# Cross attention on one core: scores by Strassen's seven products, sums of probabilities on GpSimd, and a new order of the step

## The chip, the core and the metric

The kernel runs on one core of a Trainium2 chip. The core has TensorE (PE) for matrix products, VectorE (DVE), ScalarE (ACT) and GpSimd (POOL) for elementwise work, and SyncE (SP), whose queue issues most DMAs. Each engine takes its instructions in order from a queue of its own and waits on semaphores that other engines raise. PE's results go to PSUM, which this program divides into eight banks of 128 x 512 f32; DVE and ACT read them there, and POOL works on SBUF alone. The metric is the device time of one execution in microseconds (us), smaller is better.

## The reference

The reference is one layer of a perceiver: cross attention from 8 x 64 queries to 8 x 1601 context rows, then self attention, then a feed-forward layer with weights quantised to three levels. The change lies in the cross attention, and the rest is untouched.

```python
def xattn(hidden, context, Wq, Wk, Wv, Wo, gq, gk):      # hidden 8x64x512, context 8x1601x256
    q = rmsnorm((hidden @ Wq).reshape(B, Sq, 16, 128), gq)
    k = rmsnorm((context @ Wk).reshape(B, Skv, 16, 128), gk)
    v = (context @ Wv).reshape(B, Skv, 16, 128)
    scores = einsum("bqhd,bkhd->bhqk", q, k) / sqrt(128)
    out = einsum("bhqk,bkhd->bqhd", softmax(scores), v)
    return out.reshape(B, Sq, 2048) @ Wo

x = x + xattn(layernorm(x), ctx, ...)
x = x + self_attention(layernorm(x), ...)                 # 16 heads of 32, causal
x = x + ffn(layernorm(x), ...)                            # ternary weights, 2048 hidden
```

## The kernel before

**What is computed in place of the keys.** The keys are never kept. For each head the weights of the keys are multiplied into the queries beforehand, so that a head's scores are the context (256 wide) times a matrix `a_sb` (256 x 64 for one batch and head), divided by the root of the mean square of each key. That root is the only thing for which the keys themselves are computed. Their product, context times Wk, is made by Strassen's algorithm in Winograd's form: the 256 context rows of a step and the 256 columns of the context are cut in halves, as are the 1024 columns of Wk that belong to eight heads, and seven products of 128 x 128 by 128 x 512 take the place of eight. The products need sums of the blocks of the context (`cxS`, s1 to s4, made on POOL at L204 to L207) and of the weights (`wkS`, t1, t2, t3 and n4, made once on POOL).

**Units and steps.** A unit `u` is one batch and one group of eight heads: 16 units. A unit has six steps `q` of 256 context rows each, and a tail of 65 rows that belongs to step 5. `step(u, q)` does, for its 256 rows, the seven products of the keys (`product`, L509), the squares and their sums on ACT (`squares`, L513, sixteen of 128 columns), and the scores of both tiles of 128 rows (`scores`, L478: two matmuls of 512 columns for each tile; rows on the partitions, 8 heads x 64 queries on the free axis). A step's scores are scaled by the roots at the start of the next step (`scale_pair`, put by in `later`): DVE multiplies PSUM into a tile `s` (L490) and keeps a running maximum `mx` (L499).

**The softmax lags one unit behind.** In step 0 of unit u the maxima of unit u-1 are reduced over the partitions (`find_max`: transposes L562, reduce L564) and spread to all of them by a matmul with ones (`spread_diag`, `spread_max`, L110, L556). In steps 1 to 4 (`PROBS`) each of its 13 tiles has the maximum taken off on DVE (`less_max`, L570), is exponentiated on ACT (`exponentials`, L575) and added to `den` on DVE (`add_to_sums`, L584). In step 5 the sums are spread (`find_sum`, `spread_sum`, L613) and inverted (`invert_sums`, L617). PE multiplies the tiles by the context rows into two banks `y0` and `y1` (`weigh`, `weigh_context`, L596: two matmuls of 512 columns for each tile), a few tiles later; `finish` (L623) scales the result into `a_sb`, over the queries that are no longer needed.

**What sets the order.** Inside the steps the order of PE, DVE and ACT is the order in which `step` calls, because they stand in a manual schedule. POOL and SP are ordered by the framework's scheduler. Waits follow from tiles: a writer of a buffer waits for its last reader. PSUM has these tags: `k` (two banks, p_u and p_5), `m` (two, p_2 and what is transposed or spread), `s` (two, scores), `y0` and `y1`.

The keys' products share banks. p_u is written by the first product, copied out on ACT as p1 (L718), added to by the third product and copied out as u2 (L746), added to again, read by DVE for c22 (L774), and added to a last time; p_5 is written, copied out as p5 (L743), added to and read by DVE for c12 (L803). Each of these readers has to end before PE adds to the bank again.

**Side work in the steps.** Every second step also quantises one tile of the feed-forward weights: a load `wf`, two passes on ACT (`magnitudes`, L426 and L428), five instructions on DVE at the end of the step (`quantise`, L434 to L445), three more one step later (`signed`, L451 to L453), then a DMA transpose and a store. `transpose_context` turns the context of a later step on DVE (L190) and makes its sums on POOL. `load_context` brings the rows for `weigh`, with six buffers (`CXN`). In unit 0, which has no softmax behind it, PE computes in place of `weigh` the keys' roots of the tail rows (`key_roots`: matmul L245, squares `ksq` on ACT, reduce on DVE L254).

**Before the steps** (`qphase`): the context tails are loaded in one DMA and transposed (L368), the tails' key roots of group 0 computed, x normalised and transposed, the queries computed head by head (L332) and `a_sb` formed (L358). Only PE is in a manual schedule there. **After the steps**: the last unit's softmax and `weigh`, values and projection, self attention and feed-forward.

Of the kernel before, what the change touches and what calls it, by code (L numbers as in the profile page):

```python
# [14 lines left out]
ALU = mybir.AluOpType  # L15
# [13 lines left out]
def perceiver_kernel(  # L29
# [123 lines left out]
    CXN = 6  # L153
# [14 lines left out]
    def load_blocks(b, q):  # L168

        t = ctxp.tile([P, NC, 8, 32], F32, tag="cxB", name="cxB", bufs=3)  # L170
        src = cx[b, 2 * q * P : 2 * (q + 1) * P, :].rearrange(
            "(ki kj) (c ci cj) -> ci kj c ki cj", kj=32, c=NC, cj=32
        )
        for i in range(4):
            nc.sync.dma_start(t[32 * i : 32 * i + 32], src[i])
        cxB[b, q] = t
# [7 lines left out]
    def transpose_context(b, q):  # L184
# [4 lines left out]
        t = ctxp.tile([P, NC, 2 * P], F32, tag="cxT", name="cxT", bufs=7)  # L189
# [8 lines left out]
        if (b, q) == (0, 0):  # L198
            sums = ctxp.tile([P, 4, P], F32, tag="cxB", name="cxS", bufs=3)
        else:  # L200
            sums = work.tile([P, 4, P], F32, tag="og", name="cxS", bufs=HG)
# [23 lines left out]


# [3 lines left out]
    def load_tails(qp):  # L230
        t = qp.tile([P, B, C], F32, tag="wq3", name="cxt")
        nc.sync.dma_start(
            t[:TAIL], cx[:, NJF * P :, :].rearrange("b k c -> k b c")
        )
        return t

    def key_roots(ct, g, kr, new_kp, new_ksq):
# [3 lines left out]
        ssq = small.tile([P, HG], F32, tag="ssq", name="ssq")  # L241
# [16 lines left out]
    def tail_roots(i, g, new_kp, new_ksq):  # L258
# [3 lines left out]
        kr = small.tile([P, HG], F32, tag="krt", name="krt")[: n1 - n0]  # L262
# [10 lines left out]
    with tc.tile_pool(name="qphase", bufs=1) as qp, tc.tile_pool(  # L273
# [36 lines left out]
        for q in range(2):  # L310
# [4 lines left out]
        nc.vector.scalar_tensor_tensor(  # L315
            gqk, gq_t, float(HD) ** -0.5, gk_t, ALU.mult, ALU.mult
        )
        wkT, qraw, qr = {}, {}, {}

        def transpose_wk(h):  # L320

            g, hg = divmod(h, HG)
            tp = ps.tile([P, NC, P], F32, tag="tp", name="tp_wk")
# [39 lines left out]
        with tc.manual_schedule(engines={mybir.EngineType.PE}):  # L363

            for b in range(B):
                tp = ps.tile([P, NC, P], F32, tag="tp", name="tp_cx")
                for c in range(NC):
                    nc.tensor.transpose(  # L368
                        tp[:, c, :TAIL], cxt[:TAIL, b, ts(c, P)], ident[:TAIL, :TAIL]
                    )  # L370
                (nc.scalar.copy if b % 2 else nc.vector.tensor_copy)(
                    cxP[:, :, b, :], tp[:, :, :TAIL]
                )
            load_wq(3)
            for i in range(n_tails):
                for _ in tail_roots(
# [4 lines left out]
                ):  # L381
                    pass
                if i > 0:
                    t = i - 1
                    xn = normalise(x_sb, t, qp)
                    tp = ps.tile([P, ND, P], F32, tag="tp", name="tp_ln")
                    for c in range(ND):
                        nc.tensor.transpose(tp[:, c, :], xn[:, ts(c, P)], ident)
                    nc.scalar.copy(xT[:, :, ts(t, P)], tp)
# [22 lines left out]
    def load_weights(u):  # L412
# [7 lines left out]
        wf = fq.tile([P, 512], F32, tag="wf", name="wf", bufs=2)  # L420
# [43 lines left out]
    s_sb, mx, mB, den, rB, yps = {}, {}, {}, {}, {}, {}  # L464
# [4 lines left out]
    def scores(u, j):  # L469
        b, g = divmod(u, G)  # L470
        r = rows(j)
        sp = ps.tile([P, HG, S], F32, tag="s", name="sp")
        for c in range(NC):
            if j < NJF:
                ct = cxT[b, j // 2][:, c, ts(j % 2, P)]
            else:
                ct = cxP[:, c, b, :]
            nc.tensor.matmul(  # L478
                sp[:r],
                ct,  # L480
# [4 lines left out]
        return sp  # L485

    def scale_scores(u, j, sp, kr):
        r = rows(j)
        s = work.tile([P, HG, S], F32, tag="s", name="s", bufs=16)
        nc.vector.tensor_tensor(  # L490
            s[:r], sp[:r], kr[:r].unsqueeze(2).to_broadcast([r, HG, S]), ALU.mult
        )
        s_sb[u, j] = s

# [6 lines left out]
    def bank(tag, name):  # L501
        return ps.tile([P, 4 * HD], F32, tag=tag, name=name)
# [44 lines left out]
    def spread(parts):  # L547

        bp = ps.tile([P, W], F32, tag="m", name="bp")
# [8 lines left out]
    def find_max(u):  # L558
        tp = ps.tile([P, W // P, P], F32, tag="m", name="tp_mx")
# [7 lines left out]
    def less_max(u, j):  # L567
        r = rows(j)
        s = s_sb[u, j]
        nc.vector.tensor_tensor(s[:r], s[:r], mB[u][:r], ALU.subtract)  # L570

    def exponentials(u, j):
        r = rows(j)
        s = s_sb[u, j]
        nc.scalar.activation(s[:r], s[:r], AF.Exp, bias=zero_t[:r], scale=1.0)  # L575

    def add_to_sums(u, j):
        r = rows(j)
        s = s_sb[u, j]
        if j == 1:  # L580
            den[u] = work.tile([P, HG, S], F32, tag="t2", name="den", bufs=12)
            nc.vector.tensor_tensor(den[u], s_sb[u, 0], s, ALU.add)
        elif j > 1:
            nc.vector.tensor_tensor(den[u][:r], den[u][:r], s[:r], ALU.add)  # L584

    def weigh_context(u, j):
# [7 lines left out]
        s = s_sb.pop((u, j))  # L594
        for c in range(NC):
# [51 lines left out]

    def load_wo(h):
        wo_sb[h] = work.tile([P, D], F32, tag="s", name="wo", bufs=16)
# [32 lines left out]
    PROBS = {1: range(0, 3), 2: range(3, 6), 3: range(6, 10), 4: range(10, NJ)}  # L682
# [12 lines left out]
    def step(u, q):  # L695
# [6 lines left out]
        b11, b21, b22, t1, t2_, t3, n4 = wkS[g]  # L702
        ssq = small.tile([P, 2, HG], F32, tag="ssq2", name="ssq2")
        probs = PROBS.get(q, ()) if u > 0 else ()
        sp, fw_tile = [], None
# [4 lines left out]
        p_u = bank("k", "p_u")  # L710
        product(p_u, a11, b11, True)
        if q != 1:
            for j in probs:
                less_max(u - 1, j)
        if u > 0 and q == 5:
# [3 lines left out]
        while later:  # L719
            later.pop(0)()  # L720
        if q == 1:
            for j in probs:
                less_max(u - 1, j)
# [11 lines left out]
        early = q != 1  # L735
        for j in probs[:early]:
            exponentials(u - 1, j)


        p_5 = bank("k", "p_5")  # L740
# [6 lines left out]
        for j in probs[early:]:  # L747
            exponentials(u - 1, j)
        for _ in roots:
            pass  # L750
        if u > 0 and q != 1:
            weigh(1)
        if q == NQU - 1:
            tail = scores(u, NJF)
            if u > 0:
                spread_sum(u - 1)
            scale_scores(u, NJF, tail, krP[:, b, ts(g, HG)])
        if u > 0 and q == 0:
            find_max(u - 1)
        if q % 2 == 0 and n_q < NQ:  # L760
            fw_tile = magnitudes(wf)


        c11, c22 = kept("c11"), kept("c22")

        def product_2():
            p_2 = bank("m", "p_2")
            product(p_2, a12, b21, True)
            nc.vector.tensor_tensor(c11, p_2, p1, ALU.add)
            squares(ssq[:, 0], 0, c11)  # L770

        def product_7():
            product(p_u, s3, t3, False)
            nc.vector.tensor_tensor(c22, p_u, p5, ALU.add)  # L774
            squares(ssq[:, 1], 1, c22)

        if u > 0 and q == 1:
            product_2()
            sp.append(scores(u, 2 * q))
            product_7()  # L780
        else:
            product_7()
            product_2()
            sp.append(scores(u, 2 * q))
        for j in probs:
            add_to_sums(u - 1, j)
        if u > 0 and q == 1:
            weigh(1)
        if u > 0 and q == 0:
            mB[u - 1] = spread_diag(mB[u - 1])  # L790
# [3 lines left out]
        if n_tp < len(pairs) and turn_at[n_tp] == u * NQU + q:  # L794
            transpose_context(*pairs[n_tp])
            n_tp += 1


# [537 lines left out]
```

## Time and profile before

| | |
|---|---|
| Median of 3 runs | 1744.43 us (1741.65 to 1745.04) |
| The profiled execution | 1742.82 us, of it 1741.0 us from the first to the last instruction |
| Granted TensorE clock | 0.997 on the mean |
| PE busy | 1715.9 us, 99% |
| DVE busy | 1186.6 us, 68% |
| ACT busy | 1069.9 us, 61% |
| POOL busy | 133.6 us, 8% |
| First product of the first step | at 127.2 us |

A row of a group or a timeline names the line of the program, the engine and operation, the tile that is written and those that are read, the shape and the count. In a timeline the first column is the start and the second the length from the first instruction's start to the last one's end, in us, and what stands in brackets is the idle time of the engine before it and what ended it. DVE and ACT start the next instruction some 0.08 to 0.10 us before the last one's recorded end. A matmul's recorded length is longer than the distance to the next matmul's start, because matmuls are pipelined; distances between starts are what counts. In the view of windows the columns are the window, the busy time of each engine with its count of instructions, the granted TensorE clock, and the DMA's share and rate.

### The profile page before, as it was taken

To read this page: it belongs to the slowest core of one execution; us is meant where nothing else is said; L and a number is where in the kernel's file an instruction comes from. 1 tells how busy PE (TensorE), PEld (TensorE's weight loads), DVE (VectorE), ACT (ScalarE), POOL (GpSimd) and SP (SyncE) were. 2 spreads that over 40 slices of the span, in tenths; PEclk is the share of its full clock that TensorE was granted. 3 is DMA by queue.
4 is the path that set the end of the run, shared out by engine and by line. 5 is a ranking of instruction groups with operands and counts; after the bars stand their busy time and mean duration, and the time that the engine had idled before them with its cause. 6 is when DMAs were issued, how large, how long until landed. Compare 5 with 4: busy or idle time off the path is not lost.

```text
span 1741.0 us, 17756 instructions
## 1 busy us (share of the span) xinstructions
PE 1715.9 (99%) x4712; PEld 825.6 (47%) x4712; DVE 1186.6 (68%) x2007; ACT 1069.9 (61%) x4274; POOL 133.6 (8%) x234
## 2 busy tenths in 40 slices
PE   8999999999999999999999999999999999999898
PEld 3444344444444444444444444444444444466687
DVE  4446687878787878778787878787778776145431
ACT  4447676767676776767676768676777663023441
POOL 2001100000000000000000000000000000100031
PEclk9999999999999999999999999999999999999999
DMA  6102121212121122121212212121121226400330
GB/s 194 25 7 43 37 54 45 57 39 54 46 60 46 42 57 47 49 50 46 57 40 54 53 43 57 41 59 45 46 51 31 64 50 229 132 1 1 97 97 25
DMA packets 189222, 98.76 MB, mean 57 GB/s; under 512 B 135593, under 2 KB 167873, under 8 KB 189121
## 3 DMA queue, kind: packets, MB, share of 16 engines
q1 hardware_dynamic: 182593, 85.04, 19.0%
q0 software_dynamic: 6240, 12.58, 2.8%
q8 instruction: 38, 0.62, 0.2%
q14 instruction: 63, 0.52, 0.1%
q10 hardware_dynamic: 288, 0.00, 0.0%
HBM read 77.62 MB, written 7.34 MB: 49 GB/s over the span
## 4 chain that ended last, share of the span: by engine, by line
PE 96%; ACT 2%; DVE 1%; DMA 0%; issue 0%; SPq 0%; ACTq 0%; DVEq 0%
PE y L596 21%; PE sp L478 20%; PE p_u L509 19%; PE p L509 14%; PE gu L1205 3%; PE qps L332 3%; PE op L671 3%; PE kp L245 2%; PE fop L1273 2%; PE mm_qk L990 2%; PE vp L656 2%; PE aps L358 1%; PE bp L110 1%; PE mm_v L1008 1%; ACT e L1051 1%; PE mm_p L1097 1%
## 5 line engine op out<-in xcount | busy, mean ns | idle before, releaser
L513 ACT ACTIVATE c<-c 128x128 f32<-128x128 f32 x1152 | 339.7, 296 | 104.9 <-DVE c L774 78.5
L596 PE MATMUL y<-s,cxn 128*128 128x512 f32 (+1 forms) x832 | 389.1, 592 | 0.1
L478 PE MATMUL sp<-a,cxT 128*128 128x512 f32 x768 | 360.8, 592 | 0.0
L596 PEld LDWEIGHTS y<-s,cxn 128*128 128x128 f32 (+1 forms) x832 | 158.0, 190 | 199.1 <-issue 195.9
L478 PEld LDWEIGHTS sp<-a,cxT 128*128 128x128 f32 x768 | 145.8, 190 | 178.0 <-issue 172.6
L513 ACT ACTIVATION_READ_ACCUMULATOR c<-c 128x1 f32 x1152 | 215.3, 187 | 0.0
L490 DVE TENSOR_TENSOR s<-sp,ssq 128x512 f32<-128x512 f32 x192 | 130.0, 685 | 50.1 <-ACT ssq L105 49.2
L575 ACT ACTIVATE s<-s,zero_t 128x512 f32<-128x512 f32 (+1 forms) x208 | 140.0, 716 | 7.8 <-DVE s L570 6.5
L570 DVE TENSOR_TENSOR s<-s,mB 128x512 f32<-128x512 f32 (+1 forms) x208 | 134.7, 701 | 2.1 <-ACT mB L556 2.1
L584 DVE TENSOR_TENSOR den<-den,s 128x512 f32<-128x512 f32 (+1 forms) x176 | 121.2, 689 | 12.7 <-ACT s L575 0.2
L499 DVE TENSOR_TENSOR mx<-mx,s 128x512 f32<-128x512 f32 (+1 forms) x176 | 121.7, 692 | 6.1
L513 ACT ACTIVATE p_u<-p_u 128x128 f32<-128x128 f32 x384 | 100.5, 262 | 31.4 <-PE p_u L509 22.3
L743 ACT COPY p<-p 128x512 f32<-128x512 f32 x96 | 56.2, 586 | 96.2 <-PE p L509 96.2
L803 DVE TENSOR_TENSOR c<-p,u 128x512 f32<-128x512 f32 x96 | 65.8, 686 | 68.9 <-PE p L509 66.3
L204 POOL TENSOR_TENSOR cxS<-cxT 128x128 f32<-128x128 f32 x48 | 21.9, 456 | 1170.0 <-DVE cxT L190 1103.7
L774 DVE TENSOR_TENSOR c<-p_u,p 128x512 f32<-128x512 f32 x96 | 66.2, 689 | 57.2 <-PE p_u L509 56.0
L509 PE MATMUL p_u<-wk,cxS 128*128 128x512 f32 x192 | 99.1, 598 | 0.0
L509 PE MATMUL p<-wk,cxT 128*128 128x512 f32 x192 | 98.4, 594 | 0.0
L509 PE MATMUL p_u<-wkS,cxS 128*128 128x512 f32 x192 | 98.3, 593 | 0.0
L509 PE MATMUL p<-wkS,cxS 128*128 128x512 f32 x192 | 98.2, 593 | 0.0
L509 PE MATMUL p_u<-wk,cxT 128*128 128x512 f32 x192 | 98.0, 592 | 0.0
L509 PE MATMUL p<-wk,cxS 128*128 128x512 f32 x192 | 98.0, 592 | 0.0
(174 smaller groups left out, 2397.6 us busy)
## 6 DMA issues: line engine op xcount, KB each, us to landing
cxn<-in_ctx_dram SPq DMA_DIRECT2D x192, 128.0 KB
cxB<-in_ctx_dram SPq DMA_DIRECT2D x192, 64.0 KB
wf<-in_L_ffn_w_gate_up_dram SPq DMA_DIRECT2D x32, 256.0 KB
fgu<-fw POOLq DMA_DIRECT2D x4, 2048.0 KB, 8.7
fw<-wT SPq DMA_DIRECT2D x48, 128.0 KB
wq<-in_L_xattn_Wq_dram SPq DMA_DIRECT2D x4, 1024.0 KB
wf<-in_L_ffn_w_proj_dram SPq DMA_DIRECT2D x16, 256.0 KB
wo<-in_L_xattn_Wo_dram SPq DMA_DIRECT2D x16, 256.0 KB
```

What stands on the lines that cost most here:

```text
L478: nc.tensor.matmul(sp[:r], ct, a_sb[g][c][:, :, ts(b, S)], start=(c == 0), stop=(c == NC - 1),)
L490: nc.vector.tensor_tensor(s[:r], sp[:r], kr[:r].unsqueeze(2).to_broadcast([r, HG, S]), ALU.mult)
L499: nc.vector.tensor_tensor(mx[u][:r], mx[u][:r], s[:r], ALU.max)
L509: nc.tensor.matmul(out_, a, w, start=start, stop=True, skip_group_check=not start)
L513: nc.scalar.activation(k[:, ts(h, HD)], k[:, ts(h, HD)], AF.Square, accum_out=ssq[:, 4 * half + h : 4 * half + h + 1],)
L570: nc.vector.tensor_tensor(s[:r], s[:r], mB[u][:r], ALU.subtract)
L575: nc.scalar.activation(s[:r], s[:r], AF.Exp, bias=zero_t[:r], scale=1.0)
L584: nc.vector.tensor_tensor(den[u][:r], den[u][:r], s[:r], ALU.add)
L596: nc.tensor.matmul(yps[u][c], cxn[u, j][:r, ts(c, P)], s[:r], start=(j == 0), stop=(j == NJ - 1),)
L743: nc.scalar.copy(p5, p_5)
L774: nc.vector.tensor_tensor(c22, p_u, p5, ALU.add)
L803: nc.vector.tensor_tensor(c12, p_5, u2, ALU.add)
```

## The change

Five things change together.

1. *Scores.* `scores` goes for the 12 full tiles of a unit; `tail_scores` keeps the old way for the 65 rows. The scores of a step are made by seven Strassen products of 128 x 128 by 128 x 256 with the context sums `cxS` that the keys use already. The other side's sums, t1, t2, t3 and n4 of a unit's `a_sb`, are made in `query_sums` by four POOL instructions of 128 x 256, for the next unit at the end of step 5. Six of the products go through one bank `s_a` (two halves of 256 columns), the seventh through `s_2`. Three copies on ACT and two additions on DVE put the four quarters into a tile `s` of two context tiles (128 x 1024). `s` is then scaled in place in SBUF with one DVE instruction of 1024 columns.
2. *Softmax.* `less_max` and `exponentials` take two tiles in one instruction of 1024 columns in five of the eight places, one in three. `add_to_sums` is on POOL, behind a copy of one column of `mx` into `gate`, which makes POOL wait for the step's maxima.
3. *Order of the step.* POOL joins the manual schedule. p_5 gets its second product right after the third of p_u; c12 comes before c22; p_2 comes last; p_u and p_5 are taken in turn from `k` and `m`; `later` comes after `less_max`; exponentials stand ahead of the copies of the half scores, of p_5 and of p_u on ACT.
4. *Buffers.* `CXN` 5 for 6, `cxB` 2 for 3, `cxT` 6 for 7, `wf` 1 for 2; `s` is 7 pairs in place of 16 tiles, and what used its buffers later (`wo`, `xT_lo`, `hT`) takes halves of the pairs (`piece`).
5. *Start.* The tails are loaded in four DMAs, two from SP's queue and two from ACT's. Four tails are transposed ahead of the first key roots, the first half of the key roots of all five groups of rows comes before the second half, and PE, DVE and ACT all keep the written order.

```diff
-    CXN = 6
+    CXN = 5
+    def query_sums(u):
+        b, g = divmod(u, G)
+        (b11, b12), (b21, b22) = [
+            [a_sb[g][c][:, 4 * i : 4 * i + 4, ts(b, S)] for i in range(2)]
+            for c in range(NC)
+        ]
+        t1, t2_, t3, n4 = [aT[:, i] for i in range(4)]
+        nc.gpsimd.tensor_tensor(t1, b12, b11, ALU.subtract)
+        nc.gpsimd.tensor_tensor(t2_, b22, t1, ALU.subtract)
+        nc.gpsimd.tensor_tensor(t3, b22, b12, ALU.subtract)
+        nc.gpsimd.tensor_tensor(n4, b21, t2_, ALU.subtract)
+        aS[u] = b11, b21, b22, t1, t2_, t3, n4
...
-        nc.sync.dma_start(
-            t[:TAIL], cx[:, NJF * P :, :].rearrange("b k c -> k b c")
-        )
+        for b in range(0, B, 2):
+            (nc.scalar if b % 4 else nc.sync).dma_start(
+                t[:TAIL, b : b + 2], cx[b : b + 2, NJF * P :, :].rearrange("b k c -> k b c")
+            )
...
+    def scale_scores(u, q, s, kr):
+        flat = s.rearrange("p i h s -> p (i h) s")
+        nc.vector.tensor_tensor(
+            flat, flat, kr.unsqueeze(2).to_broadcast([P, 2 * HG, S]), ALU.mult
+        )
...
-    PROBS = {1: range(0, 3), 2: range(3, 6), 3: range(6, 10), 4: range(10, NJ)}
+    PROBS = {
+        1: ((0, 1), (2,)),
+        2: ((3,), (4, 5)),
+        3: ((6, 7), (8, 9)),
+        4: ((10, 11), (12,)),
+    }
...
     p_u = bank("p_u")
     product(p_u, a11, b11, True)
+    for js in probs[:1]:
+        less_max(u - 1, js)
     p1 = kept("p1")
     nc.scalar.copy(p1, p_u)
...
+    for js in probs[1:]:
+        less_max(u - 1, js)
+    while later:
+        later.pop(0)()
+    for js in probs[:1]:
+        exponentials(u - 1, js)
+    s_a = ps.tile([P, 2, 4, S], F32, tag="s", name="s_a")
+    product(s_a[:, 0], s1, v1, True)
+    product(s_a[:, 1], a11, q11, False)
+    nc.scalar.copy(half[:, 1:3], s_a)
+    p_5 = bank("p_5")
     product(p_5, s1, t1, True)
     nc.scalar.copy(p5, p_5)
     product(p_u, s2, t2_, False)
     nc.scalar.copy(u2, p_u)
+    product(p_5, s4, b22, False)
+    product(s_a[:, 1], s2, v2, False)
+    for js in probs[1:]:
+        exponentials(u - 1, js)
+    nc.scalar.copy(half[:, 0], s_a[:, 1])
+    nc.vector.tensor_tensor(c12, p_5, u2, ALU.add)
+    squares(ssq[:, 0], 1, c12)
+    if probs:
+        nc.gpsimd.tensor_copy(gate, mx[u][:, 0, 0:1])
+    for js in probs:
+        for j in js:
+            add_to_sums(u - 1, j, nc.gpsimd)
...
     product(p_u, s3, t3, False)
     nc.vector.tensor_tensor(c22, p_u, p5, ALU.add)
     squares(ssq[:, 1], 1, c22)
+    product(s_a[:, 1], s3, v3, False)
+    product(s_a[:, 0], s4, q22, False)
+    nc.vector.tensor_tensor(quarters[:, 1::2], s_a, half[:, 0:2], ALU.add)
     product(p_u, a22, n4, False)
     squares(ssq[:, 1], 0, p_u)
+    p_2 = bank("p_2")
+    product(p_2, a12, b21, True)
+    nc.vector.tensor_tensor(c11, p_2, p1, ALU.add)
+    product(s_2, a12, q21, True)
+    nc.vector.tensor_tensor(quarters[:, 0], s_2, half[:, 2], ALU.add)
+    product(s_a[:, 1], a22, m4, False)
+    nc.scalar.copy(quarters[:, 2], s_a[:, 1])
+    squares(ssq[:, 0], 0, c11)
...
...
+        if q == NQU - 1 and u < last:
+            query_sums(u + 1)
```

## The prediction

> **What bounds the kernel now.** I read the page's totals first, then its chain, then the groups by form, and last the timelines of single steps.
>
> ```profile
> PE 1715.9 (99%) x4712; PEld 825.6 (47%) x4712; DVE 1186.6 (68%) x2007; ACT 1069.9 (61%) x4274; POOL 133.6 (8%) x234
> PE 96%; ACT 2%; DVE 1%; DMA 0%; issue 0%; SPq 0%; ACTq 0%; DVEq 0%
> PE y L596 21%; PE sp L478 20%; PE p_u L509 19%; PE p L509 14%; PE gu L1205 3%; PE qps L332 3%; PE op L671 3%; PE kp L245 2%; PE fop L1273 2%; PE mm_qk L990 2%; PE vp L656 2%; PE aps L358 1%; PE bp L110 1%; PE mm_v L1008 1%; ACT e L1051 1%; PE mm_p L1097 1%
> ```
>
> PE is busy 99% of the span and is 96% of the chain that ended last. The other engines have a third of their time free, but a share says nothing of when. So two questions decide: how much matmul time leaves, and whether what replaces it makes PE wait.
>
> The price of a matmul, from PE's timeline (columns: start, length, engine, line, tiles, count):
>
> ```profile
> 703.23 1.88 PE L478 MATMUL sp<-a,cxT 128*128 128x512 f32 x4
> 704.95 1.02 PE L509 MATMUL p_u<-wkS,cxT 128*128 128x512 f32 x2
> 1526.33 14.08 PE L990 MATMUL mm_qk<-xT_a,wa_qk 128*128 128x256 f32 x64 [0.73 <-ACT xT_a L971]
> 1540.24 3.60 PE L1008 MATMUL mm_v<-wa_vp,xT_a 128*128 128x512 f32 x8
> ```
>
> Four records of 512 columns take 704.95 - 703.23 = 1.72 us, 0.43 each; 64 records of 256 columns take 13.91 us, 0.217 each. One f32 matmul leaves two records. So 256 columns cost half of 512, and weight loads (190 ns) stay hidden at 256.
>
> The price of handing a result over, from the timeline of one step:
>
> ```profile
> 711.42 1.02 PE L509 MATMUL p<-wkS,cxS 128*128 128x512 f32 x2
> 712.28 1.02 PE L509 MATMUL p_u<-wkS,cxS 128*128 128x512 f32 x2
> 712.48 0.59 ACT L743 COPY p<-p 128x512 f32<-128x512 f32 x1 [1.45 <-PE p L509]
> 713.34 0.59 ACT L746 COPY u<-p_u 128x512 f32<-128x512 f32 x1 [0.27 <-PE p_u L509]
> ...
> 31.76 0.59 ACT L389 COPY xT_q<-tp_ln 128x512 f32<-128x512 f32 x1
> 32.40 3.70 PE L332 MATMUL qps<-xT_q,wq 128*128 128x512 f32 x8 [0.46 <-ACT xT_q L389]
> 36.16 3.60 PE L332 MATMUL qps<-xT_q,wq 128*128 128x512 f32 x8
> ```
>
> A matmul's second record starts 0.43 after its first (711.85), and the copy starts at 712.48: 0.63 later. The second pair gives 713.34 - 712.71 = 0.63 again. The way back: the copy ends at 32.35 and PE starts at 32.40, 0.05 later, and the eight records after a wait take 0.10 more than eight without (3.70 against 3.60). So a PSUM tile that PE adds to again after a reader of length R costs 0.43 + 0.63 + R + 0.05 + 0.10 = 1.21 + R us from the start of the first matmul; whatever PE has in between covers that. Before, two to four other matmuls with `scores` or `weigh` always lay between, and the waits view shows no PE wait of this kind worth naming.
>
> **The change, part by part.** There are 16 units of 6 steps. Units from the third on take 82.05 us (starts of `p_u`).
>
> 1. *Scores.* A step loses 4 matmuls of 512 (8 x 0.43 = 3.44 us) and gains 7 of 256 (14 x 0.217 = 3.04). That is 0.40 a step, 2.4 us a unit, 39 us in all if PE never waits.
>
> 2. *`p_u` read by VectorE, then added to.* c22 = p_u + p5 now has only two 256-column products (0.87) between p_u's write (0.86) and the next write of p_u. Needed: 1.21 + 0.69 (L774) = 1.90; at hand: 1.73. PE waits 0.17 in every step: 1.0 a unit.
>
> 3. *`p_5` read by ScalarE, then added to.* p_5 now gets its second product one matmul later, in place of half a step later. Needed: 1.21 + 0.59 (L743) = 1.80; at hand: 0.86 + 0.86 = 1.72. A wait of 0.08 even if ScalarE is free: 0.3 a unit, over the four steps that item 4 doesn't hold up longer.
>
> 4. *What stands ahead of the p5 copy on ScalarE.* Its queue there is now: p1 copy, root of the squares, exponentials of the first tiles, copy of the two half scores, p5 copy, u2 copy. The exponentials wait for VectorE's `less_max`, and VectorE's queue carries the quantiser's tail of an even step into the next one:
>
> ```profile
> 707.54 0.68 DVE L434 TENSOR_REDUCE tot<-aw 128x8 f32<-128x512 bf16 x1
> 708.25 0.17 DVE L436 TENSOR_SCALAR scl<-tot 128x8 bf16<-128x8 f32 x1
> 708.46 0.17 DVE L439 TENSOR_SCALAR thr<-scl 128x8 f32<-128x8 bf16 x1
> 708.66 0.69 DVE L441 TENSOR_TENSOR m<-aw,thr 128x512 bf16<-128x512 bf16 x1
> 709.27 0.69 DVE L445 TENSOR_TENSOR nd<-aw,scl 128x512 bf16<-128x512 bf16 x1
> ```
>
> These five take 2.34 us to the next start. Walk of step 3 (time 0 is its `p_u`): the quarter of the last step ends VectorE's old work at 0.3; the quantiser runs to 2.6; `less_max` of two tiles is 1024 wide. Its length isn't in the trace: 0.68 (L570, 512 wide) plus 512 columns more at the 1.04 ns that 256 against 512 wide shows (425 ns and 692 ns) gives 1.22; it ends at 3.9. The exponentials of 1024: between 0.72 (one, L575) and 1.3 (two that follow at 0.62), I take 1.15. ScalarE is at 4.9; half copy, 0.48 to the next start (as L743), 5.4; p5 copy 5.4 to 6.0; PE goes on at 6.1 and was ready at 5.15: 0.95 lost. In step 1 `less_max` starts 0.5 sooner (the quantiser began while PE spread the maxima): 0.5 to 0.6 lost. Steps 2 and 4 have no quantiser in front and only item 3's 0.08. Sum: 1.5 a unit.
>
> So a full unit loses 1.0 + 0.3 + 1.5 = 2.8 us and saves 2.4: 0.4 slower, 82.4. Over 14 units (two to fifteen): +5.5.
>
> 5. *Unit 0.* No exponentials, but the tail's key roots: VectorE's reduction of `ksq` and the transpose now stand ahead of c22 in its queue, and ScalarE makes `ksq` only after the four squares of c12. With 0.69 (reduce) and 0.61 (transpose) in front, c22 starts 1.2 late. Five steps x 1.3 = 6.5 lost, against 2.4 saved and some 0.9 of small waits that the unit has now (first records 0.1 longer behind the key roots, one gap in its last step): +3.2.
>
> 6. *Unit 1.* It had one wait of 2.20 us (tp_mx on DVE mx) and 3.4 us at half clock behind it: 81.06. The transposes are now later, but step 1's exponentials wait 2 us for the first maxima: about 81.8, +0.7.
>
> 7. *First loads in quarters, new order.* Before, PE started at 6.28 on the tails' load and reached the dense `kp` at 10.68. The first quarter is there some 2 us sooner and `kp` waits only for the weights (POOL's first sum of wk starts at 8.90, so they have landed by then). Two quarters are issued from ScalarE's queue, ahead of gq and gk, whose product now comes after the first `kp`. But VectorE and ScalarE now keep the written order, and the last `tp_ln` waits for its `xn`. A gain of 3 at the front, 2 given back: -1, between -3.5 and +1.
>
> 8. *Tail.* CXN 5 in place of 6: load j+5 starts when tile j is used, 5 x 1.72 = 8.6 us ahead of its use. The first such load at the tail stands behind w_attn and x (3 MB): its predecessor came just in time. +1.2, from 0 to 4. The last maxima reach PE later, as fewer matmuls lie behind them: +1.3.
>
> 9. *Sums on GpSimd.* 128x512 takes 1.26 to 1.33 us (L220 to L223), so four take 5.2 us of a 13.7 us step, from the maxima at 7.6 to 12.9; the sums of context (4 x 0.46) follow, used steps later; `query_sums` of 256 columns lie between 0.46 and 1.27, some 0.73 each. Cost 0: the cover is the time to `find_sum` in step 5. It holds until an add takes twice as long. VectorE loses 0.69 x 12 a unit, which was idle time there. Wf with one buffer, cxB with two, cxT with six: each load is still issued after a reader that ended a step before, 0.
>
> For item 9 a rule speaks against the change. Row: `m` L453, median 425 ns, is up to 567 when a GpSimd sum lies over it, and the 128x128 sum of L206 has a median of 462 ns and a most of 641.
>
> ```profile
> L453 DVE TENSOR_TENSOR m<-nd,m x48: 424/425/567, 152.8 to 1431.7; 128x512 bf16<-128x512 bf16 x48
> ```
>
> The Trainium skill (GPSIMD Engine Reference, Specifications) says that GpSimd shares its SBUF interfaces with VectorE and contends with instructions that have two SBUF inputs or run in a two-port mode. By the rule only `less_max`, scaling and maxima would suffer; the adds run beside c12, the transpose, c22 and the quarters, which read PSUM or one input. I add nothing; by the row (a third longer wherever adds lie over VectorE) c22 would take 0.92 and each of four steps 0.23 more: +15 us.
>
> Sum: 5.5 + 3.2 + 0.7 - 1 + 2.5 = +10.9. The profiled execution took 1742.8 (span 1741.0), so 1753.7; the median of the three runs is 1.6 above it: about 1755.
>
> **The rivals.**
> - *The saving stays.* If the turnarounds of items 2 to 4 cost half (the exponentials in time on ScalarE, above all), the units save 1 us each and unit 0 breaks even: about 1730; without any wait 1705. It decides from where a unit's waits fall under the 2.4 us saved, so item 4 under 1.1. For it: before, PE waited for nothing. Against: 0.63, 0.69 and 1.73 are measured. Chance 0.08.
> - *A draw*, 1741 to 1748: item 4 a third smaller. Chance 0.10. A measurement of this kernel can tell about 0.2%, 3.5 us, from no change.
> - *As summed*: 1748 to 1765. Chance 0.60.
> - *Contention or late exponentials*, 1765 to 1785: VectorE's queue 3 to 8% slower moves every `less_max` and c22, and each 0.1 us a step is 10 us. Chance 0.17.
> - *The clock gives way*, 1785 and more: the clock fell to half for 3.4 us after 2.20 us idle at 208.8. 30 steps with a wait near 1 us would cost 1.7 each, 51 us. Against: a window idle for 37% kept its clock.
>
> ```profile
> 208.59:212.00 3.41, 3.23 (x7) 1.92 (x8) 1.19 (x3) 0.00 (x0) 0.00 (x0) 0.50 0.30 77
> ...
> 1618.30:1621.60 3.30, 2.08 (x11) 1.13 (x9) 1.79 (x6) 3.10 (x17) 0.00 (x0) 1.00 1.50 403
> 1621.70:1625.10 3.40, 2.82 (x33) 2.19 (x34) 1.10 (x3) 1.52 (x3) 0.00 (x0) 1.00 0.36 90
> ```
>
> Step 3 idles 1.1 of 3.4, a third. Chance 0.05. The range 1743 to 1774 leaves out the first rival, and the upper half of the last two.
>
> **What would show it.** In the profile after: PE's matmul time down by some 39 us, and PE with idle time of about 45 us in the steps, ahead of `p_5` on ScalarE and of `p_u` on VectorE c22, each step with 0.17; step 3 the longest of those without extra work. Units of 82.4. Wrong if units come below 81.5 (waits smaller), or above 83.5 (VectorE or GpSimd slowed: `less_max` over 1.3 us or `den` over 1.5), or if the clock shows halves in the units.

## Result and profile after

The changed kernel takes 1766.14 us (median of 4 runs, 1758.7 to 1767.27) against 1744.74 before: ratio 1.0118, 95% interval 1.0087 to 1.0148. The profiled execution took 1765.5 us, its span is 1763.5, so 22.5 more than the span of before. The forecast was slower, 1755.

The totals and the chain of the kernel after:

```profile
PE 1713.7 (97%) x5288; PEld 917.9 (52%) x5288; DVE 1153.5 (65%) x1848; ACT 1154.3 (65%) x4487; POOL 412.8 (23%) x538
...
PE 82%; DVE 11%; ACT 5%; DMA 1%; issue 1%; SPq 0%; DVEq 0%; ACTq 0%
PE y L665 17%; PE p_u L570 16%; PE p L570 13%; PE s_a L570 11%; PE gu L1298 3%; PE qps L346 3%; PE op L751 3%; ACT s L643 2%; DVE s L639 2%; PE fop L1366 2%; PE mm_qk L1083 2%; PE s L570 2%; PE vp L736 2%; PE aps L372 1%; PE sp L518 1%; PE kp L262 1%
```

PE's share of the chain falls from 96% to 82%. What VectorE and ScalarE gained there is work of theirs that ends in a wait of PE; it is not the length of the waits, for PE is busy beside most of it (PE's idle time is 49.8 us, before 25.1). The groups that came in are the exponentials (ACT s L643) and the subtraction of the maxima (DVE s L639), the work that item 4 put ahead of the p5 copy. PE's busy time fell by only 2.2 us where 39 us of matmuls left. A record of 512 columns is drawn 0.59 long at a pitch of 0.43, so its overhang paints over waits of up to 0.16 us, and the 0.10 by which a product behind a wait is late is drawn as busy too: the busy share can't be used to count short waits, the starts can.

Where the 22.5 us lie, by the starts of `p_u`:

| stretch | before | after | difference | forecast |
|---|---|---|---|---|
| up to the first `p_u` | 127.18 | 128.74 | +1.6 | -1 |
| unit 0 | 76.57 | 84.02 | +7.45 | +3.2 |
| unit 1 | 81.06 | 81.46 | +0.4 | +0.7 |
| units 2 to 14 (13) | 82.05 each | 82.90 each | +11.05 | +0.4 each |
| from unit 15 on | 389.6 | 391.6 | +2.0 | +0.4, +2.5 |

Step 3 of a full unit is the walk of item 4. Its time 0 is the `p_u` at 584.50. From the timelines of VectorE, ScalarE and PE after (start, length, engine, line, tiles; in brackets the idle time before and who ended it):

```profile
585.90 0.69 DVE L486 TENSOR_TENSOR m<-aw,thr 128x512 bf16<-128x512 bf16 x1
586.51 0.69 DVE L490 TENSOR_TENSOR nd<-aw,scl 128x512 bf16<-128x512 bf16 x1
587.12 2.35 DVE L639 TENSOR_TENSOR s<-s,mB 128x1024 f32<-128x1024 f32 x2
```
```profile
588.37 1.15 ACT L643 ACTIVATE s<-s,zero_t 128x1024 f32<-128x1024 f32 x1 [1.10 <-DVE s L639]
589.42 0.56 ACT L835 COPY half<-s_a 128x512 f32<-128x512 f32 x1
589.89 0.59 ACT L839 COPY p<-p 128x512 f32<-128x512 f32 x1
```
```profile
584.50 1.02 PE L570 MATMUL p_u<-wk,cxT 128*128 128x512 f32 x2
...
588.80 1.02 PE L570 MATMUL p_u<-wkS,cxS 128*128 128x512 f32 x2
590.53 1.13 PE L570 MATMUL p<-wk,cxS 128*128 128x512 f32 x2 [0.70 <-ACT p L839]
...
594.93 0.59 PE L570 MATMUL s_a<-a,cxS 128*128 128x256 f32 x2
595.44 1.12 PE L570 MATMUL p_u<-wkS,cxT 128*128 128x512 f32 x2
```

The quantiser runs to 2.6, `less_max` starts at 2.62, the exponentials at 3.87, the p5 copy runs from 5.39 to 5.98 and PE goes on at 6.03. The prediction had 2.6, 2.6, 3.9, 5.4 to 6.0 and 6.1. PE could have gone on at 588.80 + 0.86 = 589.66: 0.87 lost (the view shows 0.70 of it, the rest lies under the overhang), and the second record comes 0.10 late behind it. The second wait is in the last two lines: 595.44 - 594.93 = 0.51 where two 256-column records take 0.43: 0.08, and the next product starts 0.10 late as well (596.40 instead of 596.30). That is the c22 turnaround.

### The profile page after: what moved, and what is told of

The parts are those of the page before. It is cut to its first block, busy times and chain, and to the rows that moved or that the text cites. A ratio compares the mean times of both kernels' runs of the same rounds, so it can differ in the third digit from the quotient of the medians.

```text
span 1763.5 us, 19431 instructions
## 1 busy us (share of the span) xinstructions
PE 1713.7 (97%) x5288; PEld 917.9 (52%) x5288; DVE 1153.5 (65%) x1848; ACT 1154.3 (65%) x4487; POOL 412.8 (23%) x538
## 4 chain that ended last, share of the span: by engine, by line
PE 82%; DVE 11%; ACT 5%; DMA 1%; issue 1%; SPq 0%; DVEq 0%; ACTq 0%
PE y L665 17%; PE p_u L570 16%; PE p L570 13%; PE s_a L570 11%; PE gu L1298 3%; PE qps L346 3%; PE op L751 3%; ACT s L643 2%; DVE s L639 2%; PE fop L1366 2%; PE mm_qk L1083 2%; PE s L570 2%; PE vp L736 2%; PE aps L372 1%; PE sp L518 1%; PE kp L262 1%
## 5 line engine op out<-in xcount | busy, mean ns | idle before, releaser
L665 PE MATMUL y<-s,cxn 128*128 128x512 f32 x768 | 356.7, 592 | 1.7 <-DMA cxn<-in_ctx_dram 1.7
L665 PEld LDWEIGHTS y<-s,cxn 128*128 128x128 f32 x768 | 144.7, 190 | 146.6 <-issue 139.9
L652 POOL TENSOR_TENSOR den<-den,s 128x512 f32<-128x512 f32 x150 | 190.5, 1270 | 8.2
L570 PEld LDWEIGHTS s_a<-aT,cxS 128*128 128x128 f32 x576 | 109.3, 190 | 132.5 <-issue 117.3
L570 PE MATMUL s_a<-aT,cxS 128*128 128x256 f32 x576 | 171.4, 379 | 0.0
L643 ACT ACTIVATE s<-s,zero_t 128x1024 f32<-128x1024 f32 (+1 forms) x117 | 116.7, 998 | 32.8 <-DVE s L639 32.8
L639 DVE TENSOR_TENSOR s<-s,mB 128x1024 f32<-128x1024 f32 (+1 forms) x117 | 117.3, 1025 | 2.1 <-ACT mB L617 2.1
L539 DVE TENSOR_TENSOR s<-s,ssq 128x1024 f32<-128x1024 f32 x96 | 116.0, 1209 | 1.8 <-ACT ssq L105 1.5
L570 PE MATMUL p_u<-wkS,cxT 128*128 128x512 f32 x192 | 108.0, 645 | 8.0 <-DVE c L880 8.0
L555 DVE TENSOR_TENSOR mx<-mx,s 128x512 f32<-128x512 f32 x160 | 111.1, 694 | 6.5
```

The costliest lines, as they stand in the source:

```text
L539: nc.vector.tensor_tensor(flat, flat, kr.unsqueeze(2).to_broadcast([P, 2 * HG, S]), ALU.mult)
L555: nc.vector.tensor_tensor(mx[u][:r], mx[u][:r], s[:r], ALU.max)
L570: nc.tensor.matmul(out_, a, w, start=start, stop=True, skip_group_check=not start)
L639: nc.vector.tensor_tensor(t, t, m.to_broadcast([r, len(js), W]), ALU.subtract)
L643: nc.scalar.activation(t, t, AF.Exp, bias=zero_t[: t.shape[0]], scale=1.0)
L652: eng.tensor_tensor(den[u][:r], den[u][:r], s[:r], ALU.add)
```

## Experiments

All are edits of the changed kernel; their times stand against 1766.14. "Unit" is the mean pitch of units 3 to 13 (82.9 in the changed kernel).

**First: the exponentials behind the p5 copy.**

```
-        for js in probs[:1]:
-            exponentials(u - 1, js)
...
         nc.scalar.copy(p5, p_5)
+        for js in probs[:1]:
+            exponentials(u - 1, js)
```

> The exponentials of a step's first tiles are moved behind the p5 copy in ScalarE's queue; nothing else changes. If the p5 copy comes late because the exponentials stand ahead of it (theory), PE's waits at the second product of p_5 fall from 0.40, 0.9 and 0.2 us in steps 1, 3 and 4 to 0.08 or less, a unit from the third on comes down by about 1.5 us to 81.4, and the kernel by 15 x 1.5 = 22 us, to about 1744. The 0.09 + 0.10 us at p_u behind c22 stay. If VectorE is slowed by GpSimd's sums and that is what holds the units (rival), the waits only move to another product and the gain is under 5 us.

Measured: 1738.05 us, ratio to before 0.9972 (0.9959 to 0.9985). Unit 81.4; step 3 12.76 after 13.65, step 1 14.45 after 14.87, step 4 12.76 after 12.94. The waits at c22 are as they were, 0.08 to 0.09 and 0.10. Timeline of PE in step 3: the second product of p_5 now follows at its pitch of 0.86, with 0.08 lost inside it, as in the steps without a quantiser:

```profile
578.94 1.02 PE L570 MATMUL p_u<-wkS,cxS 128*128 128x512 f32 x2
579.79 1.11 PE L570 MATMUL p<-wk,cxS 128*128 128x512 f32 x2
```

So 1.5 us of a unit hung on the place of one group of exponentials in ScalarE's queue, the size of item 4. (The 28 us are more than the 22 expected: units 2 to 14 give 19.5, unit 1 gives 2.7 and what follows from unit 15 on 3.6; 2.2 lie ahead of the first `p_u`, where nothing was changed.)

**Second: another product in the c22 turnaround.**

```
-        product(p_u, a22, n4, False)
-        squares(ssq[:, 1], 0, p_u)
         p_2 = bank("p_2")
         product(p_2, a12, b21, True)
+        product(p_u, a22, n4, False)
         c11 = kept("c11")
...
+        squares(ssq[:, 1], 0, p_u)
```

> p_2's product (two records of 512 columns, 0.86 us) is put ahead of the last product added to p_u, so that more PE work lies between c22's read of p_u and the next write. If the c22 turnaround is the wait (theory), 0.17 to 0.19 us a step go, 1.0 to 1.1 us a unit, and in unit 0, where the waits were 1.04 us in four steps, 0.82 and 2.56 in the last two, about 0.96 us a step: 15 x 1.05 + 5.5 = 21 us less, about 1745; units at 81.9, unit 0 near 78. If instead VectorE as a whole is too late because of GpSimd (rival), the wait comes back at c11 or at the quarters of the next step and the gain is under 8 us.

Measured: 1738.82 us, 0.9961 (0.9947 to 0.9975). Unit 81.5, unit 0 79.1. In full units the wait at this place is gone, and step 2, which has no other disturbance, takes 12.55 after 12.74: 0.19. In steps 0 to 2 of unit 0 the wait falls from 1.04 to 0.18. In the full units VectorE was not late elsewhere: no new wait took its place. (Of the 27 us, 3.3 lie ahead of the first `p_u`, where nothing was changed. The unit lost 1.4, where 1.0 to 1.1 was expected, because the p5 waits of steps 1 and 3 fell by some 0.15 each as well, while that of step 4 grew by 0.1.)

**Third: another product in the p5 turnaround.**

```
-        product(p_5, s4, b22, False)
         product(s_a[:, 1], s2, v2, False)
+        product(p_5, s4, b22, False)
```

> The product s2 x v2 (two records of 256 columns, 0.43 us) is put ahead of p_5's second product. Theory: each p_5 wait shrinks by up to 0.43 us plus the 0.10 behind it: step 1 from 0.40 to 0, step 3 from 0.9 to 0.45, step 4 from 0.2 to 0, the other steps by 0.08: about 1.0 to 1.3 us a unit, 14 to 20 us in all, 1746 to 1752. If the copy is held by something that moves with PE, the wait stays as it is and nothing is gained.

Measured: 1745.81 us, 1.0010 (1.0002 to 1.0019). Unit 81.7, step 3 13.22 after 13.65, step 2 12.65 after 12.74. The wait in step 3 shrinks by the 0.43 that was put in its way, and the steps with 0.08 lose it. What is left of it stands at another place: the product that was moved ahead writes to `s_a` and waits for the copy of the half scores, which lies in ScalarE's queue just ahead of the p5 copy and behind the same exponentials.

```profile
583.81 0.70 PE L570 MATMUL s_a<-aT,cxS 128*128 128x256 f32 x2 [0.22 <-ACT half L835]
584.35 1.08 PE L570 MATMUL p<-wk,cxS 128*128 128x512 f32 x2
```

ScalarE's copies are late by a fixed time of its own, not by a time that moves with PE.

**Fourth: all three.**

> All three moves together. If the three waits are separate terms of one sum (theory), the gains add: 22 + 21 + about 4 (what is left of the p_5 waits) = 45 to 48 us, units at 79.5, the kernel at 1718 to 1722, so some 24 us faster than before the change. If VectorE or GpSimd has become the bound behind those waits (rival), the units stop at 81 or more and the time stays above 1740.

Measured: 1712.93 us, 0.9817 (0.9802 to 0.9832), unit 79.9. Timeline of PE in step 3:

```profile
580.27 1.02 PE L570 MATMUL p_u<-wkS,cxS 128*128 128x512 f32 x2
581.13 0.59 PE L570 MATMUL s_a<-aT,cxS 128*128 128x256 f32 x2
581.56 1.02 PE L570 MATMUL p<-wk,cxS 128*128 128x512 f32 x2
...
585.86 1.02 PE L570 MATMUL p<-wk,cxT 128*128 128x512 f32 x2
586.72 1.02 PE L570 MATMUL p_u<-wkS,cxT 128*128 128x512 f32 x2
587.58 0.59 PE L570 MATMUL s<-a,cxT 128*128 128x256 f32 x2
```

Each start lies 0.86 (512 columns) or 0.43 (256) behind the one before it: no wait at all. Steps 2, 3 and 4 take 12.46 where they took 12.88 before the change. That 0.42 is the whole saving of item 1 (forecast 0.40): the seven products do what they promise once the handovers are covered, with the same matmuls as in the changed kernel. The kernel is 53 us faster than the changed one, more than the 45 to 48 expected, though a unit came down a little less (79.9, expected 79.5): 3.7 of the 53 lie ahead of the first `p_u`, where nothing was changed, and 4.2 in unit 1.

**Fifth: GpSimd's weight sums out of unit 0.** Of the four sums for the second group of weights, three are issued in the query phase:

```
                 if h == HG:
                     weight_sums(0)
+                    weight_t3(0)
+                    weight_sums(1)
...
         if u == 0 and q == NQU - 2:
-            weight_sums(1)
+            weight_t3(1)
```

(`weight_t3` is the sum that overwrites its input, `b12 = b22 - b12`, taken out of `weight_sums`.) The reason is step 5 of unit 0 in the kernel after, timelines of VectorE, GpSimd and PE:

```profile
199.06 1.19 DVE L484 TENSOR_SCALAR thr<-scl 128x8 f32<-128x8 bf16 x1
200.29 1.71 DVE L486 TENSOR_TENSOR m<-aw,thr 128x512 bf16<-128x512 bf16 x1
201.92 1.21 DVE L490 TENSOR_TENSOR nd<-aw,scl 128x512 bf16<-128x512 bf16 x1
```
```profile
198.96 1.26 POOL L222 TENSOR_TENSOR wk<-wk 128x512 f32<-128x512 f32 x1
200.19 1.26 POOL L223 TENSOR_TENSOR wkS<-wk,wkS 128x512 f32<-128x512 f32 x1
201.41 1.17 POOL L236 TENSOR_TENSOR aT<-a 128x256 f32<-128x256 f32 x1
```
```profile
208.71 1.12 PE L570 MATMUL p_u<-wkS,cxT 128*128 128x512 f32 x2 [2.39 <-DVE c L880]
209.67 1.60 PE L570 MATMUL p<-wk,cxT 128*128 128x512 f32 x2
```

A `thr` of 128x8, 0.17 us elsewhere, lasts until GpSimd's sum ends, and the next two instructions are held by the next two sums. c22 comes 2.56 us late, and the records behind it have twice their pitch: the granted clock is half from 209.98 to 213.40.

> Undoes nothing of the change but the place of GpSimd's weight sums for the second group: three of the four 128x512 sums are issued in the query phase, only the one that overwrites its input stays at the end of step 4 of unit 0. Theory: in the changed kernel VectorE's quantiser, scaling and maxima of unit 0's step 5 were held by these sums (thr 1.19 us for 0.17, m 1.71 for 0.69, nd 1.21 for 0.69, two maxima 1.83 for 1.29: 3.1 us in all), which made c22 late and PE idle for 2.56 us, after which the clock fell to half for 3.4 us. With two of these instructions free of a sum, c22 comes 1 to 2 us sooner, the wait falls to 0.8 to 1.5 us, the half clock goes or shrinks, and unit 0 falls from 84.0 to 80 to 82.5: 2 to 4 us in all. Rival: the stretched rows have another cause (code, PSUM, the DMA of the weights); then unit 0 stays at 84.

Measured: 1761.7 us, 1.0108 (1.0090 to 1.0126). Unit 0 80.33 after 84.02; the same wait is 0.25 (PE starts at 202.86, ready at 202.61), the quantiser has its 0.69 again, and the clock stays full. So 3.7 us of unit 0 came from these sums: 2.3 as a wait, the rest at half clock.

**Sixth: the sums of probabilities without the gate.** The copy on GpSimd that waits for the maxima is taken out:

```
-        if probs:
-            nc.gpsimd.tensor_copy(gate, mx[u][:, 0, 0:1])
```

> GpSimd's copy that waits for a step's maxima (the gate) is left out, so the sums of probabilities start as soon as their exponentials are there, 2 to 3 us sooner, over VectorE's scaling and maxima. If VectorE is held by GpSimd only where both of its inputs lie in SBUF (the rule weighed in the prediction), the maxima grow from 0.69 to 0.9 to 1.2 us and the scaling from 1.22 to 1.6 or more in the steps with sums, while c12, c22 and the quarters keep 0.69; since VectorE idles 1.4 us ahead of c22 in those steps, the units grow by 1 us at most: 1764 to 1780. If contention lies over every VectorE instruction (the bound), c22 and c12 also take 0.9. If there is none (rival), no row changes, and the time is within 3 us.

Measured: 1769.49 us, 1.0148 (1.0120 to 1.0177), unit 83.0. The instructions by line (minimum, median and maximum in ns), of the kernel after first:

```profile
L555 DVE TENSOR_TENSOR mx<-mx,s x160: 680/692/1102, 161.5 to 1459.9; 128x512 f32<-128x512 f32 x160
L880 DVE TENSOR_TENSOR c<-p_u,p x96: 639/691/693, 139.0 to 1451.0; 128x512 f32<-128x512 f32 x96
L497 DVE TENSOR_TENSOR m<-m,sg x48: 415/671/951, 156.8 to 1455.1; 128x512 bf16<-128x512 bf16 x48
```

and without the gate:

```profile
L555 DVE TENSOR_TENSOR mx<-mx,s x160: 682/1202/1652, 160.1 to 1460.9; 128x512 f32<-128x512 f32 x160
L876 DVE TENSOR_TENSOR c<-p_u,p x96: 640/692/693, 137.7 to 1452.0; 128x512 f32<-128x512 f32 x96
L497 DVE TENSOR_TENSOR m<-m,sg x48: 418/420/954, 155.5 to 1456.0; 128x512 bf16<-128x512 bf16 x48
```

The median of the maxima mixes two groups. The 75 of them over which a sum of probabilities lies take 1.64 each; nearly all of the other 85 keep 0.69. Both of their inputs lie in SBUF. GpSimd's own sums take 1.60 instead of 1.27 (medians), and 14 of the 96 scalings (L539) 2.3 instead of 1.22. That is more than was expected (0.9 to 1.2 for the maxima). c22, one of whose inputs lies in PSUM, keeps 0.69, in the 30 steps too in which a sum lies over it. In step 3 PE's wait for c22 grows by some 0.35 us, in step 4 the p5 wait of 0.2 goes, because GpSimd is done sooner and leaves the quantiser's `m` of the next step alone (median 420 ns, 671 with the gate). The two nearly cancel.

**Seventh: the sums on VectorE.** `add_to_sums(u - 1, j, nc.vector)` and no gate.

> The sums of probabilities go back to VectorE (without the gate), in the place where GpSimd's are issued: after c12, ahead of c22. Theory (GpSimd's sums cost nothing, item 9): VectorE gets 12 x 0.69 = 8.3 us a unit more ahead of c22, of which it had about 1.4 us free in a step with sums; c22 is then up to 1.3 us late in the steps with four sums, units grow by about 1 us, 1775 to 1782. Rival (GpSimd's sums are what makes the units 82.9 instead of the 82.4 forecast): the units get shorter, under 82.5, and the kernel faster than 1760.

Measured: 1781.09 us, 1.0215 (1.0192 to 1.0238), unit 84.2. In step 3 PE waits 1.3 us for c22, which stands behind four sums:

```profile
594.29 0.68 DVE L848 TENSOR_TENSOR c<-p,u 128x512 f32<-128x512 f32 x1
594.89 2.93 DVE L652 TENSOR_TENSOR den<-den,s 128x512 f32<-128x512 f32 x4
597.74 0.70 DVE L190 STREAM_TRANSPOSE cxT<-cxB 128x512 f32<-128x512 f32 x1
598.36 0.65 DVE L876 TENSOR_TENSOR c<-p_u,p 128x512 f32<-128x512 f32 x1
```

GpSimd as the place of the sums is worth about 15 us against this placement; the sums are not what made the change slower.

**Eighth: what follows from all of it.** The fourth kernel with the weight sums of the fifth, the second half of unit 0's key roots moved behind c22, and the first block of wk loaded ahead of the last two quarters of the tails:

```
-        for _ in roots:
-            pass
...
         squares(ssq[:, 1], 1, c22)
+        for _ in roots:
+            pass
...
+        load_tails(cxt, range(0, 4, 2))
+        load_wk(0, 0)
+        load_tails(cxt, range(4, B, 2))
```

> All three moves of the fourth run, with the weight sums of the fifth, the key roots' second half in unit 0 moved behind c22 (so that VectorE's reduction of ksq no longer stands ahead of it), and the load of the first wk block issued ahead of the last two quarters of the tails. Theory: unit 0 from 81.25 to 76 to 77.5 (waits of 0.52 us in four steps and of 3.2 in the last one go, and the half clock behind it), other units as in the fourth run, 79.9; the start sooner by 0 to 1.5: 1705 to 1709. If the waits of unit 0 come from elsewhere, it stays at 1711 to 1714.

Measured: 1709.28 us, 0.9803 (0.9788 to 0.9817): faster than both kernels. Unit 0 is 76.1 (81.25 in the fourth run), as expected, but by other parts than expected. Nearly all of it, 4.9 us, lies in step 5 (10.91 after 15.83), where the wait of 3.2 for c22 and the half clock behind it go with the weight sums, as in the fifth run. Behind c22 the key roots gain next to nothing: steps 0 to 4 together take 65.2 after 65.4. PE's waits of 0.42 to 0.61 for c22 in steps 0 to 3 are gone, so VectorE's reduction of `ksq` was their cause, and steps 1 and 3 take 12.46. But in steps 0, 2 and 4, where ScalarE has the quantiser's two passes ahead of `ksq`, the reduction now comes late and holds up the addition of the quarters behind it, for which PE waits 0.43 to 0.83. Timelines of VectorE and PE in step 0:

```profile
137.25 0.69 DVE L273 TENSOR_REDUCE ssq<-ksq 128x4 f32<-128x512 f32 x1 [2.84 <-ACT ksq L272]
137.85 0.68 DVE L890 TENSOR_TENSOR s<-s_a,half 128x512 f32<-128x512 f32 x1
```
```profile
137.41 0.59 PE L576 MATMUL s<-a,cxT 128*128 128x256 f32 x2
138.68 0.67 PE L576 MATMUL s_a<-aT,cxT 128*128 128x256 f32 x2 [0.67 <-DVE s L890]
```

The new order of the loads shows no gain either: the first `p_u` lies at 125.8, 125.1 in the fourth run. The intervals of the two runs overlap, and none of the three edits was run alone on top of the fourth kernel.

## Why the prediction came out as it did

The direction and its reason hold: the saving is real, and it is more than spent on handovers that the new order leaves uncovered. The time itself lies 11 us above the forecast, just inside the rival "contention or late exponentials" (from 1765), and part of the 11 us is that rival's mechanism. It is in the stated range without luck in the sum, for the large errors do not cancel: by the profiles the start, unit 0 and the full units cost 2.6, 4.2 and 5.8 us more than forecast, unit 1 and the end 1.2 less. (The range is described wrongly: with 1774 at its top it leaves out the last rival, from 1785, as a whole.) By its steps:

- *Item 1* (0.40 a step saved): 0.42, in the fourth run.
- *Item 2* (c22, 0.17 a step): 0.09 and 0.10. The second run took 0.19 from a step.
- *Items 3 and 4* (p5 copy, exponentials): 0.08 in steps 0 and 2, up to 0.14 in step 5; 0.86 to 0.96 in step 3 and 0.40 in step 1, these two with 0.07 to 0.10 more behind them, as worked out. Mis-sized is step 4, taken at 0.08: it lost 0.3. The prediction put no quantiser ahead of `less_max` there, but the second half of the quantiser (L496 to L498) is, and its `nd` and `m` are stretched from 0.42 to 0.68 and 0.67 by GpSimd's sums of the context, which come behind those of the probabilities. VectorE and GpSimd, the kernel after:

```profile
598.40 0.68 DVE L496 TENSOR_TENSOR nd<-aw,nd 128x512 bf16<-128x512 bf16 x1
599.01 0.67 DVE L497 TENSOR_TENSOR m<-m,sg 128x512 bf16<-128x512 bf16 x1
```
```profile
598.88 0.52 POOL L207 TENSOR_TENSOR cxS<-cxT,cxS 128x128 f32<-128x128 f32 x1
```

  The first and third run show this whole group as the price of one order of two queues.
- *A full unit* (82.4): 82.9. Waits of 3.2 us in place of 2.8, of it 0.2 by step 4, the rest in small terms: 82.05 - 2.4 + 3.2 = 82.85. Over 13 units this is 5.8 of the missing 11 us.
- *Item 5, unit 0* (+3.2): +7.45. The wait of about 1.04 in steps 0 to 3 was foreseen (1.3 with the restart). Step 5 was not: 3.7 us by the fifth run, from GpSimd's weight sums and the half clock that followed. The diff showed GpSimd put under a hand-written order. In the profile of before three of these four sums run at 19.8 to 23.8 us, in the query phase; the prediction walked through the queues of VectorE and ScalarE in their new order, and left GpSimd's out.
- *Item 6, unit 1*: +0.4 for +0.7. The wait in step 1 came as forecast (PE waits 2.1 us for the p5 copy, 2 expected), and the clock stayed full behind it.
- *Item 7, start* (-1): +1.6 in this profile. Six of the other runs have the same loads and the same query phase; their first `p_u` lies at 125.1 to 127.4, with this one 126.6 on average, 0.5 sooner than in the one profile of before. The first matmul came 2.2 sooner, as forecast, and then PE waited for the first wk block, 1.56 to 3.97 us. Timelines of PE, the kernel after and the fourth run:

```profile
9.37 3.75 PE L262 MATMUL kp<-wk,cxP 128*128 128x512 f32 x4 [3.97 <-DMA wk<-in_L_xattn_Wk_dram]
```
```profile
6.78 3.75 PE L262 MATMUL kp<-wk,cxP 128*128 128x512 f32 x4 [1.56 <-DMA wk<-in_L_xattn_Wk_dram]
```

  "Landed by then" was the failing step: it was read from a start of 8.90 on GpSimd, and the quarters stand ahead of wk in the queue now. A term of 2 us at the start can't be judged by one profile.
- *Item 8, tail*: +2.0 with the last unit for 2.9, its DMA wait 1.7 for 1.2, the wait for the last maxima 0.9 for 1.3. From unit 15 on, the profiles of the changed kernel and its edits differ by up to 4.6 us (388.0 to 392.6), so this term can't be judged closely.
- *Item 9, sums on GpSimd* (0): the sums themselves yes, against VectorE (seventh run), but not free: 0.2 a unit in step 4. The rule of the Trainium skill weighed there (GPSIMD Engine Reference, Specifications) holds in its place: in the sixth run the maxima (two inputs in SBUF) took 1.64 and c22 (one in PSUM) 0.69 under the same sums, and in unit 0 bf16 instructions were held until a sum ended. The prediction drew the right list of instructions from it and then looked only at the sums of probabilities. The bound from the row of before, a third longer everywhere, was wrong: nothing that reads PSUM grew, and the maxima more than doubled.
- *The clock*: the waits near 1 us, in step 3 of the full units (0.86 to 0.96) and in steps 0 to 4 of unit 0 (0.82 to 1.04), cost no clock, as argued. In the units it gave way once, in unit 0.

## What to carry to other kernels

When a change thins out the work on the engine that bounds, list every tile that it writes again after another engine has read it, and count the work between the two writes against write + handover + reader + return; here 1.90 us against 1.73 cost 0.19 in each step of the full units, and one product swapped in paid it back. On the reader's queue, put the instruction that frees the bounding engine's tile ahead of anything that waits for a third engine. And when a second elementwise engine gets work, ask at each place which of the first one's instructions with two SBUF inputs, and which like `thr`, lie under it.

## What was not expected of the hardware

*How hard a sum on GpSimd holds VectorE.* `thr`, 128x8, took 1.19 us for 0.17, while `tot`, a reduction with one input in SBUF, kept its 0.68 beside the sum before it. The Trainium skill (SBUF — State Buffer, Who interferes with whom) describes the shared ports as a lock for a whole instruction, so that the order of issue and not the size decides who waits. The rows agree for `thr`: where it started 0.02 us ahead of a sum, in the kernel before, it kept its 0.17. The prediction had weighed a third more.

*The clock goes by a fixed grid, not by the length of a wait.* In the second run PE idled longer at this place (2.79 us) than in the kernel after (2.39), and kept the full clock:

```profile
202.79 1.12 PE L570 MATMUL p_u<-wkS,cxT 128*128 128x512 f32 x2 [2.79 <-DVE c L880]
```

The changes of the granted clock lie on a grid of 3.41 us that has another phase in each run (in the kernel after at 209.98, 213.40, 1646.99 and 1653.82, which are 1, 420 and 2 steps of 3.413 apart). On that grid, windows of the kernel after and then of the second run (the stretch; then its length and the busy time with the count of instructions on PE, weight loads, VectorE, ScalarE and GpSimd; granted clock; DMA share; GB/s):

```profile
206.57:209.98 3.41, 1.27 (x3) 0.68 (x4) 2.65 (x5) 1.89 (x13) 0.14 (x1) 1.00 0.00 0
209.98:213.40 3.42, 3.42 (x7) 2.02 (x6) 1.90 (x5) 2.33 (x14) 0.28 (x1) 0.50 0.00 0
```
```profile
198.43:201.84 3.41, 1.56 (x6) 0.66 (x4) 3.34 (x5) 0.00 (x0) 0.98 (x2) 1.00 0.00 0
201.84:205.25 3.41, 2.46 (x8) 1.63 (x9) 2.96 (x7) 3.05 (x20) 0.33 (x1) 1.00 0.00 0
```

In the kernel after the wait lies in one window, PE is busy for 1.27 us of it, and the next window has half the clock. In the second run the grid cuts the wait: 1.56 and 2.46 busy, and nothing falls. The other profiles fit: in the kernel before (in unit 1), the kernel after and the first, third, fourth, sixth and seventh run, a window in these units with PE busy for 0.9 to 1.4 us was followed by half clock, and neither the one with 1.56 was nor, in unit 1 of the kernel after, one with 1.69 and a wait of 1.95. The Trainium skill (TensorE: Matmul & The Clock Gate, Part 1: The HAM clock gate) has the free-running window of 3.41 us, with a drop after an idle window; here a window that was idle for about 60% was enough. The busy share alone is not the rule, though. Behind the units, the window from 1628.53 of the kernel before, with 1.59 busy, was followed by half clock and that from 1626.28 of the first run, with 1.59 busy too, was not; in the kernel before even one with 2.38 was (from 1645.60). What else decides stays open. In unit 0 a wait of 2.4 to 3.1 us cost its own time alone (second run), or about 1.7 us more (an estimate: half of one window, as in the kernel after), or up to twice that (fourth run, 6.83 us at half clock).
